# A gated two-layer block on one core: the alignment in two parts of 16 sequences, the second part's beside the first part's experts

## The chip, the cores and the metric

The kernel runs on one core of one Trainium2 chip. The time is device microseconds of one execution. Before the change three executions took 896.85, 896.81 and 893.13 us: the median is 896.81 us. The profiled execution took 894.79 us, of which 892.8 us lie between its first and its last instruction (the span); its mean granted TensorE clock is 0.857.

## What is computed

The input is 32 sequences of 128 tokens with 128 features. Two layers of two blocks follow, cut here to their core:

```python
x = x + tanh(g_xattn[0]) * mlstm(layernorm(x), ctx, ctx)       # 8 heads
x = x + tanh(g_ffn[0])   * qlinear(gelu(qlinear(layernorm(x), W1, b1)), W2, b2)
x = x + tanh(g_xattn[1]) * align(ctx, layernorm(x))
x = x + tanh(g_ffn[1])   * moe(layernorm(x))

def qlinear(x, W, b):      # both quantised to 8 bits over the WHOLE tensor
    xq, sx, zx = affine_quantize(x); wq, sw = sym_quantize(W)
    return (xq - zx) @ wq.T * (sx * sw) + b

def align(small, large):   # for each sequence by itself
    D = pairwise_euclidean(small, large)           # 128 x 128
    R[i, j] = D[i, j] + min(R[i-1, j], R[i, j-1], R[i-1, j-1])
    # walk back from the last corner; sum the rows of small met at each column
    return zeros_like(large).at[path_j].add(small[path_i])

def moe(x):                # 8 experts, all of them for every token
    logits = x @ gate.T
    kth = sort(logits.reshape(-1))[3072 - 1]       # over ALL 32 sequences
    gates = logits * (logits >= kth)
    y = gelu(x @ w1.T + b1) @ w2.T + b2            # per expert, 128 -> 512 -> 128
    return sum_e(gates[e] * y[e])
```

Two things couple the sequences. The scale of the second dense product needs the largest and smallest value of all of its inputs, and the gates need one threshold, the 3072nd smallest logit of all sequences. An expert's output for a token can be computed before the threshold is known, but it can only be weighted after it.

## The kernel before

A tile holds 128 tokens of a sequence on the 128 partitions, or its features. Sequences are taken in 8 groups of 4. The stages run in this order, each over all 32 sequences:

1. The first block (heads), then the first dense product. Its outputs after the gelu stay in `HT`, and their extremes give the scale of the second product.
2. The second dense product, `dense(n)` for group n. VectorE scales a block of 128x2048 (L865), ScalarE clips it from below (L868), VectorE from above (L869), TensorE makes 16 products into `po` (L874), and VectorE adds them to `X` (L879). Two groups at a time are then normalised (`norm_steps`) and turned (`tp`).
3. The distances, `take(g)`. ScalarE makes `ym2` and `ysq` (L884, L886), TensorE the squared distances `d2` (L888, L890), ScalarE adds a bias (L897) and takes the root (L899, L900), and DMAs put the rows into `d_dram` (L902).
4. The warp. A sequence is walked from both ends at once, so each of 64 partitions holds one half of one sequence and there are 64 rows of 128 columns. A row is two instructions on VectorE (L991, L992), one behind the other. Rows come in chunks of 16, 16, 16, 8 and 8, and the loads `dc` bring each chunk's distances. After a chunk its rows are spread by DMA over 128 partitions (`rblk`, two blocks of half a chunk), where five instructions find which way the path went (`dg`, `lf`, `to`, `vv` and `dv`, L1017 to L1029). `dv` goes back to 64 partitions by DMA (`DV`, L1031). ScalarE takes one part of it, a copy of the first column (L1028). At the last row the two halves meet (`meet`, L945 to L968), with two products on TensorE. Then 63 instructions `hit` (L1038) walk the path back, each needing the one before. `vt` and `ends` turn the result into the range of rows that each column takes.
5. The experts. `aligned(g)` adds the aligned context to group g (`ge`, `pt`, `px`), normalises it, turns it into `YT` (L1099) and computes its logits (L1102). A *unit* here means one group through one expert: 4 products `mph` of 128x512 (L1162), 4 gelus on ScalarE (L1165) and 16 products `mpo` of 128x128 (L1171). Groups are the outer loop, experts the inner one, 64 units in all. Groups 2 to 7 are aligned between the first units. The threshold is found bit by bit in 31 steps (`search`) among the units of group 1: each step is a count on VectorE, a product on TensorE (`small`, L1116) and three small instructions on VectorE. The outputs of groups 0 and 1 are held on chip (`ye`). From group 2 on `combine` adds each output to `X` with its gate: four instructions for the bias and four for the product, 128x128 each (L1150).

The weights of all 8 experts lie on chip (`mw1s` and `mw2s`, loaded at L751 and L752).

An instruction waits in its engine's queue behind those before it, and TensorE, VectorE and ScalarE take their queues in order. The order in a queue is the scheduler's, made when the kernel is built. `tc.issue_after(i)` only adds that what the block traces on i's engine stands behind i in that queue: it is no wait. DMAs that are issued from one engine stand in that engine's queue as well, and an issue waits there for the data, for the buffer, and for one of eight semaphores of the DMAs.

Of the kernel before, what the change touches and what calls it, by code (L numbers as in the profile page):

```python
# [18 lines left out]
P = 128  # L19
B = 32  # L20
# [14 lines left out]
CHUNKS = ((0, 16), (16, 16), (32, 16), (48, 8), (56, 8))  # L35


@with_exitstack
def tile_flamingo_gated(
# [23 lines left out]
    def pool(stack, name, bufs=1, space=None):  # L63
        kw = {} if space is None else {"space": space}
        return stack.enter_context(tc.tile_pool(name=name, bufs=bufs, **kw))
# [17 lines left out]
    w1s = new(keep, [P, HID], F32, "w1s")  # L83
    w2s = new(keep, [P, NC, D], F32, "w2s")
# [663 lines left out]
    late = pool(ctx, "late")  # L748
    mw1s = new(late, [P, E, HID], F32, "mw1s")
    mw2s = new(late, [P, E, NC, D], F32, "mw2s")  # L750
    nc.sync.dma_start(out=mw1s, in_=mw1)  # L751
    nc.sync.dma_start(out=mw2s, in_=mw2)  # L752


    aa_s = new(keep, [P, B], F32, "aa_s")
    d_dram = new(dram, [2, B, SH, S], F32, "d_dram")
    with ExitStack() as st:
        fp = pool(st, "ffn")
        HT = new(fp, [P, NC, B * S], F32, "HT")

        def lowest(lo, tag):

            low = new(fp, [P, 2], F32, tag)
            nc.vector.tensor_scalar(low[:, 1:2], lo, -1.0, None, ALU.mult)
            return low, nc.vector.tensor_scalar(low[:, 0:1], lo, MAGIC, None, ALU.subtract)
# [11 lines left out]
        with ExitStack() as st2:  # L777
            xp = pool(st2, "xq")
            p_h = pool(st2, "p_h", bufs=2, space=PSUM)
            cp = pool(st2, "context", bufs=2)  # L780
# [23 lines left out]
            for n in range(4):  # L804
                for c in range(NC):
# [7 lines left out]
                    hb = HT[:, c, 1024 * n : 1024 * n + 1024]  # L813
# [23 lines left out]
        aa = new(fp, [P, B], F32, "aa")  # L837
        with ExitStack() as st2:
            fps = pool(st2, "ffnps2", space=PSUM)
            mm = max_everywhere(fp, fps, hs2, 2, "mmh")  # L840
            sh, inv, lo, hi = affine_scale(fp, mm, "qh")
# [7 lines left out]
        s2 = new(fp, [P, 1], F32, "s2")  # L849
# [4 lines left out]
        ties = [tie, tie]  # L854


        dp = pool(st, "dist", bufs=2)
        lp = pool(st, "ln", bufs=2)
        p_o = pool(st, "p_o", bufs=2, space=PSUM)
        dps = pool(st, "distps", bufs=2, space=PSUM)  # L860

        def dense(n):
            blk = HT[:, :, 512 * n : 512 * n + 512]
            with tc.issue_after(getattr(ties[n], "ins", ties[n])):
                nc.vector.tensor_scalar(blk, blk, inv, MAGIC, ALU.mult, ALU.add)  # L865
            yield
            hq = new(dp, [P, NC, 512], BF16, "hqt")
            nc.scalar.activation(hq, blk, AF.Relu, bias=low[:, 1:2])  # L868
# [372 lines left out]
```

## Time and profile before

| | before |
|---|---|
| median of three executions | 896.81 us |
| profiled execution, its span | 894.79 us, 892.8 us |
| granted TensorE clock, mean | 0.857 |
| TensorE busy (matmuls) | 672.7 us, 75% of the span |
| VectorE busy | 548.7 us, 61% |
| ScalarE busy | 387.8 us, 43% |
| GpSimd busy | 19.4 us, 2% |
| HBM read, written | 14.01 MB, 4.46 MB |

Stages, by the timeline: the scaling of the second dense product starts at 226.5 us, its last distance DMA is issued at 287.9 us, the first row of the warp scans at 293.8 us and the last ends at 362.8 us, the walk back runs from 373.05 to 397.4 us, the first `mph` starts at 413.06 us and the last `mpo` ends at 888.3 us.

A busy share is read together with the stage that it belongs to: TensorE's 75% is an average over a stage in which it is nearly idle and one in which it never stops. In the lines of groups, "idle before" is the time that the engine stood still just before such an instruction, with what ended most of it.

### The profile page before, as it was taken

The numbers are of one execution on the slowest core, as the hardware profiler recorded it, in microseconds if no ns is written. First come the engines' busy times: TensorE is split into PE (matmuls) and PEld (weight loads), VectorE is DVE, ScalarE is ACT, GpSimd is POOL, SyncE is SP. The second block draws the span as 40 slices with busy tenths as digits, with TensorE's granted clock in tenths as the row PEclk, the third lists the DMA queues.
The fourth block names the chain that finished last, engine by engine and source line by source line (L and its number), as shares of the span: only waits on it lengthen the run. The fifth ranks groups of instructions, "written<-read, shape, count | busy, mean of one in ns | idle before, by whom it ended". The sixth has DMA issues, their size and how long they took to land.

```text
span 892.8 us, 12600 instructions
## 1 busy us (share of the span) xinstructions
PE 672.7 (75%) x4682; PEld 454.9 (51%) x4682; DVE 548.7 (61%) x1943; ACT 387.8 (43%) x672; POOL 19.4 (2%) x52
## 2 busy tenths in 40 slices
PE   5789998242475000017999999999999999999997
PEld 2244554110353000015777667777777777777776
DVE  7768988889882799786663556995222333222332
ACT  2788774595477000002443444334443344333342
POOL 2000000004000000000000000000000000000000
PEclk9899987555578555556999999999999999999999
DMA  8100000400013535100000000000000000000000
GB/s 314 35 2 12 2 2 1 189 0 0 1 24 72 126 85 113 42 0 1 1 1 1 1 1 1 13 1 25 1 13 1 1 12 1 12 1 1 13 1 12
DMA packets 11943, 25.32 MB, mean 28 GB/s; under 512 B 2386, under 2 KB 7250, under 8 KB 11090
## 3 DMA queue, kind: packets, MB, share of 16 engines
q1 hardware_dynamic: 9880, 20.19, 7.4%
q10 hardware_dynamic: 1874, 4.23, 2.1%
q8 instruction: 36, 0.59, 0.3%
q14 instruction: 25, 0.20, 0.1%
q0 software_dynamic: 128, 0.10, 0.0%
HBM read 14.01 MB, written 4.46 MB: 21 GB/s over the span
## 4 chain that ended last, share of the span: by engine, by line
PE 52%; DVE 21%; ACT 3%; issue 2%; DMA 1%; ACTq 0%; DVEq 0%; POOLq 0%
PE mpo L1171 25%; PE mph L1162 22%; DVE ru L992 3%; DVE hit L1038 3%; DVE hst L818 2%; DVE hst L819 2%; DVE ru L991 2%; PE d L888 1%; DVE bn L147 1%; PE d L890 1%; PE small L1102 1%; PE po L874 1%; DVE pt L1086 1%; ACT dd L897 1%; PE px L1089 1%
## 5 line engine op out<-in xcount | busy, mean ns | idle before, releaser
L1171 PEld LDWEIGHTS mpo<-mw2s,hT 128*128 128x128 f32 x2048 | 252.2, 192 | 62.5 <-issue 39.2
L1165 ACT ACTIVATE hT<-mph,mb1s 128x512 f32<-128x512 f32 x256 | 175.9, 687 | 238.4 <-PE mph L1162 236.7
L1171 PE MATMUL mpo<-mw2s,hT 128*128 128x128 f32 x2048 | 256.5, 276 | 0.1
L1162 PE MATMUL mph<-YT,mw1s 128*128 128x512 f32 x512 | 243.8, 599 | 0.0
L1150 DVE SCALAR_TENSOR_TENSOR X<-mpo,GA,X 128x128 f32<-128x128 f32 x192 | 54.0, 343 | 198.1 <-PE mpo L1171 198.1
L1162 PEld LDWEIGHTS mph<-YT,mw1s 128*128 128x128 f32 x512 | 87.8, 193 | 62.1 <-issue 62.0
L1150 DVE SCALAR_TENSOR_TENSOR X<-mb2s,GA,X 128x128 f32<-128x128 f32 x256 | 73.1, 342 | 0.0
L945 PE MATMUL gt_ps<-ident,ru 32*128 32x32 f32 x1 | 0.3, 283 | 78.3 <-DVE ru L992 78.3
L945 PEld LDWEIGHTS gt_ps<-ident,ru 32*128 32x128 f32 x1 | 0.2, 178 | 78.5 <-issue 78.5
L1028 ACT COPY dv<-vv 128x8 bf16<-128x8 bf16 (+1 forms) x5 | 1.1, 220 | 78.0 <-DMA rblk<-ru 48.3
L554 ACT ACTIVATE dm<-bi 128x512 f32<-128x512 f32 x48 | 28.7, 601 | 11.8 <-issue 4.2
L596 DVE TENSOR_TENSOR sm<-sc,dm 128x512 f32<-128x512 f32 x32 | 21.7, 684 | 13.3 <-ACT dm L554 9.3
L992 DVE TENSOR_TENSOR_SCAN ru<-ru,dc 64x128 f32<-64x128 f32 x64 | 26.6, 416 | 5.0 <-DMA dc<-d_dram 3.0
L809 PE MATMUL ph<-XQ,w1q 128*128 128x512 bf16 x32 | 15.4, 602 | 17.5 <-DVE XQ L800 9.5
L1099 ACT COPY YT<-px 128x512 f32<-128x512 f32 x8 | 4.7, 585 | 49.8 <-PE px L1098 49.8
L868 ACT ACTIVATE hqt<-HT,low 128x2048 bf16<-128x2048 f32 x8 | 15.8, 2000 | 22.2 <-DVE HT L865 14.0
L1179 ACT COPY ye<-mpo 128x512 f32<-128x512 f32 x16 | 9.4, 585 | 35.5 <-PE small L1116 18.1
L1044 PE MATMUL vt<-ident,vw 64*64 64x64 f32 x1 | 0.3, 312 | 32.3 <-DVE hit L1038 32.3
L1038 DVE SCALAR_TENSOR_TENSOR hit<-jotab,vw,DV 64x128 bf16<-64x128 bf16 x63 | 21.7, 344 | 4.6 <-DMA DV<-dv 2.4
L874 PE MATMUL po<-w2q,hqt 128*128 128x128 bf16 x128 | 13.4, 278 | 13.6 <-DVE hqt L869 13.6
L510 ACT ACTIVATE qm<-YT,mcol 128x512 f32<-128x512 f32 x32 | 23.1, 728 | 0.0
L147 DVE BATCH_NORM_STATS2 bn<-X 128x6 f32<-128x128 f32 x96 | 22.0, 280 | 0.1
(314 smaller groups left out, 912.1 us busy)
## 6 DMA issues: line engine op xcount, KB each, us to landing
X<-in_x SPq DMA_DIRECT2D x4, 512.0 KB, 6.1
CD<-in_ctx_d SPq DMA_DIRECT2D x4, 512.0 KB, 7.0
CT<-in_ctx_t SPq DMA_DIRECT2D x4, 512.0 KB, 9.2
mw1s<-in_mw SPq DMA_DIRECT2D x1, 2048.0 KB, 7.8
mw2s<-in_mw SPq DMA_DIRECT2D x1, 2048.0 KB, 12.2
out_x<-X SPq DMA_DIRECT2D x8, 256.0 KB, 2.0
d_dram<-dist SPq DMA_DIRECT2D x15, 128.0 KB, 2.4
rblk<-ru ACTq DMA_DIRECT2D x6, 297.0 KB, 4.3
```

The costliest lines, as they stand in the source:

```text
L147: nc.vector.bn_stats(bn[:, i, :], v[:, i, :])
L510: nc.scalar.activation(held["qm", g][:, h], YT[:, GB * g : GB * g + GB, :], AF.Copy, scale=mcol[:, h : h + 1],)
L554: done = nc.scalar.activation(dm, bi, AF.Exp)
L596: got = nc.vector.tensor_tensor(sm, scs[:, u], dm, ALU.mult)
L818: nc.vector.tensor_reduce(hst[:, 0, o : o + 1], hb, AX.X, ALU.max)
L874: nc.tensor.matmul(po[:, i, :], lhsT=hq[:, c, i * S : (i + 1) * S], rhs=w2q[:, c, :], start=(c == 0), stop=(c == NC - 1),)
L992: nc.vector.tensor_tensor_scan(ru[:, r + 1, 0, 1 : S + 1], u, dc[:, r, :], BIG, ALU.min, ALU.add)
L1038: nc.vector.scalar_tensor_tensor(hit, jotab[0:H2], vw[:, r + 1 : r + 2], DV[:, r, :], ALU.is_le, ALU.mult, accum_out=vw[:, r : r + 1],)
L1150: nc.vector.scalar_tensor_tensor(X[:, b, :], v, gate, X[:, b, :], ALU.mult, ALU.add)
L1162: nc.tensor.matmul(ph, lhsT=mw1s[:, e, c * P : (c + 1) * P], rhs=tok, start=True, stop=True)
L1165: nc.scalar.activation(hT[:, c, :], ph, AF.Gelu_apprx_tanh, bias=mb1s[:, e, c : c + 1])
L1171: nc.tensor.matmul(po[:, i, :], lhsT=hT[:, c, i * S : (i + 1) * S], rhs=mw2s[:, e, c, :], start=(c == 0), stop=(c == NC - 1),)
```

## The change

The 32 sequences are cut into two parts of 16 from the second dense product on. The first part goes through the second dense product, distances and warp, as before. Then the expert units begin with groups 0 to 3, and the second part's dense product, distances, warp, `aligned(4)` to `aligned(7)` and the search are put among them: a generator `background()` hands out these steps, and after each gelu and each output block of a unit `pump(0.85)` takes steps of about that many microseconds, by weights that are written beside each `yield`. The warp has as many rows and walk-back steps for 16 sequences as for 32, so there are two of them. The outputs of the first 36 units wait in DRAM (`y_dram`), with the bias already added by GpSimd, and are loaded again (`yl`) once the gates are known; from unit 36 on `combine` adds the bias to all four blocks at once and then does four instructions.

Other parts of it: expert weights come in pairs of experts through two buffers, and each pair is loaded twice (pair outer, groups inner). `rblk` has four blocks of a quarter of a chunk in place of two of a half, so the five instructions are half as long and the DMAs are twice as many. `DV` lies in `YT` or `CD`, and `DV` and `dc` are set to zero by GpSimd first. In the second part all of these DMAs are issued from SP, `po`, `tp` and `d2` share two banks of PSUM (`px`), and the roots of all four groups are two instructions of 64x2048.

```diff
+BP = B // 2
+NP = NG // 2
+BL = 4
+HELD = 36
...
-    mw1s = new(late, [P, E, HID], F32, "mw1s")
-    mw2s = new(late, [P, E, NC, D], F32, "mw2s")
-    nc.sync.dma_start(out=mw1s, in_=mw1)
-    nc.sync.dma_start(out=mw2s, in_=mw2)
+    def expert_weights(p):
+        w = new(late, [P, 2, HID], F32, "mw1"), new(late, [P, 2, NC, D], F32, "mw2")
+        for to, src in zip(w, (mw1, mw2)):
+            nc.sync.dma_start(out=to, in_=src[:, 2 * p : 2 * p + 2])
+        return w
+    weights = [expert_weights(0), expert_weights(1)]
...
+    def distances(s0, dd, dist, queues):
+        nc.scalar.activation(dist[0:SH], dd[0:SH], AF.Sqrt)
+        nc.scalar.activation(dist[SH:P], dd[SH:P, :, ::-1], AF.Sqrt)
...
+    def warp_steps(s0, n_s, wp, w1p, ps_new, queues, DV, ends):
+        nc.gpsimd.memset(DV, 0.0)
+        dcs = [new(w1p, [H2, 16, S], F32, f"dc{k}") for k in range(2)]
+        for dc in dcs:
+            nc.gpsimd.memset(dc, 0.0)
...
-            m = n // 2
-            rb = new(w1p, [P, 9, 2, S + 4], F32, "rblk")
-            for q in range(2):
+            m = n // BL
+            rb = new(w1p, [P, 16 // BL + 1, 2, S + 4], F32, "rblk")
+            for q in range(BL):
                 for h in range(2):
+                    at = 2 * n_s * q + n_s * h
                     queues[h].dma_start(
-                        out=rb[H2 * q + B * h : H2 * q + B * h + B, 0 : m + 1],
-                        in_=ru[B * h : B * h + B, q * m : q * m + m + 1],
+                        out=rb[at : at + n_s, 0 : m + 1],
+                        in_=ru[B * h : B * h + n_s, q * m : q * m + m + 1],
                     )
...
+        def second_part():
...
+                for w in dense_steps(1, held["aligned", NP - 1], dp, lpB, px_new, p_x, "px", take):
+                    yield w
+                distances(BP, dd, dist, (nc.sync, nc.sync))
+                yield 2.0
...
+                for w in warp_steps(
+                    BP, BP, wp, w1p, lambda shape, tag: new(p_k, shape, F32, "small"),
+                    (nc.sync, nc.sync), DV, ends[1],
+                ):
+                    yield w
+            for g in range(NP, NG):
+                for w in aligned(g):
+                    yield w
+            for w in search():
+                yield w
...
+        def pump(more):
+            time[0] += more
+            while time[0] > 0:
+                with ExitStack() as ties:
+                    for k in ("mm", "gelu"):
+                        ties.enter_context(tc.issue_after(held[k]))
+                    w = next(steps, None)
+                if w is None:
+                    return
+                time[0] -= w
...
+        def combine_early():
+            g, e, k = early.pop(0)
+            yl = new(yp, [P, GB, D], F32, "yl")
+            nc.sync.dma_start(out=yl, in_=y_dram[k])
+            combine(g, e, yl, True)
...
+        units = [
+            (k, p, g, j)
+            for k in range(2) for p in range(E // 2) for g in range(NP * k, NP * k + NP) for j in range(2)
+        ]
+        for n, (k, p, g, j) in enumerate(units):
...
+            if n < HELD:
+                ye = new(yp, [P, GB, D], F32, "ye")
+                nc.scalar.copy(ye, po)
+                nc.gpsimd.tensor_add(ye, ye, mb2s[:, e : e + 1, :].to_broadcast([P, GB, D]))
+                nc.sync.dma_start(out=y_dram[n], in_=ye)
+                early.append((g, e, n))
+            else:
+                until("GA")
+                for _ in range(-(-len(early) // (len(units) - n))):
+                    combine_early()
+                combine(g, e, po, False)
+            if g % NP == NP - 1 and j == 1:
+                weights.pop(0)
+                if n + 2 * NP < len(units) - 1:
+                    weights.append(expert_weights((p + 2) % (E // 2)))
```

## The prediction

> **What bounds the kernel now.** I read the time slices first, then the busy times of four stretches, then the groups, the timeline around the places where work will move, and last the order in which the built program of the changed kernel has its instructions in each queue (it holds no times).
>
> ```profile
> PE   5789998242475000017999999999999999999997
> DVE  7768988889882799786663556995222333222332
> PEclk9899987555578555556999999999999999999999
> ```
> ```profile
> 226.00:290.00 64.00, 38.24 (x240) 29.10 (x240) 43.35 (x156) 43.75 (x73) 0.72 (x5) 0.71 0.16 33
> 290.00:373.00 83.00, 0.92 (x3) 0.36 (x3) 69.84 (x168) 1.54 (x7) 0.86 (x7) 0.50 0.45 99
> 373.00:400.00 27.00, 1.53 (x6) 1.10 (x6) 23.42 (x134) 0.00 (x0) 0.00 (x0) 0.50 0.00 1
> 620.00:700.00 80.00, 80.00 (x466) 58.74 (x465) 23.17 (x86) 30.68 (x45) 0.00 (x0) 1.00 0.01 4
> ```
> Columns of the stretches: length, busy us of TensorE, its weight loads, VectorE, ScalarE, GpSimd, granted clock, DMA share, GB/s. VectorE alone sets the pace from 290 to 400 us, TensorE alone from 413 us: 80.00 of 80.00 us busy at clock 1.00. The expert stage is a wall: a unit recurs every 7.006 us (573.36, 580.37, 587.38 in the chain), so 64 units are 448.4 us of the 475.1 between 413.06 and 888.2. Whatever moves into this stage must fit beside TensorE, and whatever TensorE does for it is added in full.
>
> **Ahead of the experts: what goes.** (a) Half of the second dense product and distances. Eight groups take 226.5 to 287.9. I replay the first four with these rows: a scaling 1.28, `hqt` on ScalarE 2.00 and VectorE 0.75, two `d2` from 248.81 to 254.25 at the half clock, the rest as in the timeline. Up to 241 us nothing changes; then VectorE loses 1.9 us of groups 4 and 5, the second pair no longer waits for 2.00 us pieces of `hqt`, and the last root ends at about 265.9. **−22.0.**
>
> (b) The first part's warp has its 64 rows, 0.78 us each, and its 63 `hit` unchanged. Its block instructions halve: for 16 rows 1.19+1.21+0.68+2.28+0.68 = 6.0 become the 3.3 that 8 rows cost today (0.68+0.67+0.41+1.19+0.41). Three chunks save 2.7 each, and the fourth chunk's block now stands behind the last row: rows end 11.1 earlier. But the meeting gets longer:
> ```profile
> 362.87 0.52 ACTq L1002 DMA_DIRECT2D rblk<-ru  x1
> 362.99 0.28 PE L945 MATMUL gt_ps<-ident,ru 32*128 32x32 f32 x1 [78.30 <-DVE ru L992]
> 370.75 0.51 ACTq L1031 DMA_DIRECT2D DV<-dv  x1
> 373.05 0.34 DVE L1038 SCALAR_TENSOR_TENSOR hit<-jotab,vw,DV 64x128 bf16<-64x128 bf16 x1 [2.39 <-DMA DV<-dv]
> ```
> Today the last `rblk` is issued as the rows end, and the first `hit` starts 10.1 us later. In the new order `rblk` has one buffer still, and the last chunk's eight DMAs may only start when the fourth chunk's `lf` has read it, some 3.9 us after the last row; among them, on both queues, stand four `DV` issues that wait for `dv` (about 6 us). With 0.51 an issue they are out at 8.9, land 2.4 later, the last block takes 2.2, four more `DV` issues 2.0 and 2.0 to land: first `hit` at 17.5. +7.4, so **−3.7** (ends: −11, if the meeting hides it all, and +4).
>
> (c) `aligned(1)` leaves the start: its products stand between 410.3 and 413.06, of which 0.9 go. **−0.9.** GpSimd's clearing of `DV` (8192 values; 0.94 for 1024, so 7.5) stands ahead of the 9.25 us of bias added to `X` at 213.97; it then ends at 230.8, and the first reader is at 233.65. Hidden by 2.8 us.
>
> **Beside the experts: what comes.** (d) TensorE's own part of the second dense product: per group 16 `po` 0.95 (row at 254.25: 1.06), four turns 0.55, `d2` 0.86 and 0.9 (starts at 282.77 and 283.63), 3.4 in all. Four groups: **+13.6.** Nothing can hide it.
>
> (e) ScalarE in units 4 to 8 of the new order: 16 gelus of 0.69, four `hqt` of 2.0, eight `ym`/`ysq` of 0.5, 16 biases of 0.26, the roots and the copies: 37 us in some 42 of TensorE's. It fits, but gelus queue behind it. Worst at unit 8: biases 1.0, table load, two roots of 64x2048 (2.1 each, as 128x2048 costs 2.00), a copy 0.5, a table load, then the next gelu.
> ```profile
> 253.65 2.02 ACT L868 ACTIVATE hqt<-HT,low 128x2048 bf16<-128x2048 f32 x1
> 255.68 1.28 ACT L899 ACT_TABLE_LOAD   x1
> 256.97 0.63 ACT L899 ACTIVATE dist<-dd 64x512 f32<-64x512 f32 x1
> ```
> That is 9 us without a gelu; `mph` has three buffers, so TensorE has 1.8+2.6 us of work and stands 4.8. The Trainium skill (ScalarE: Activation LUTs, What ACT_TABLE_LOAD costs) speaks against such a pair of switches: each is 1.28 of load plus 1.38 of drain, 2.66. Here the root starts 1.29 after the load began and `hqt` had ended before, so I see no drain and take 1.28; by the rule the wait would be 7.5. For the other queueing I take 2.8 (0 to 8). **+7.6.**
>
> (f) The second warp is placed from unit 9 to unit 27. VectorE's work there would fit, but all DMAs now stand in SP's queue in a fixed order: eight `rblk`, the next `dc`, eight `DV`, with `y_dram` stores between. Each `DV` waits for a ScalarE copy that stands at gelu 13.25, 17.5, 20.5, 22.5 and 23.5 (in units); behind the third `DV` stand the fourth `rblk` and, behind it, the last `dc`. From the roots' end at unit 8 (time 0): third copy 89.4, eight `DV` 93.4, eight `rblk` 97.4, `dc` lands 100.9, eight rows and a block: 107.8. TensorE reaches the meeting's first product (its place is unit 23.25) at 103.4 and waits 4.4; ScalarE's queue waits with it. From there to the first `hit`: 12.5 (today's 10.1, plus four more issues); walk 24.5; TensorE has 89 `mpo` of 0.223 and 15 `mph` of 0.86, 33.8 with the meeting, and waits 3.8 more at `vt`. **+8.2** (0 to 30).
>
> (g) One more aligned group in the stage (2.9, by 9.93 against 7.006 for a unit with one, less 1.4 already there): +1.5. The search costs 0.72 a unit today over 8 units; in the new order five steps stand in a unit and some follow after 1.12 us where the steps at 499.99 and 501.46 need 1.47: +0.8. From `ends` to the first `px`: +1.5. **+3.8.**
>
> (h) Held outputs: 33 loads come right after the search, up to 4.75 between two `combine`. 4.75 times 1.06 for four instructions, plus 0.74 and 1.06, is 6.8 of 7.0 us; with three buffers and 2.0 to land a load recurs after about 1.35, so 8.1. PSUM holds two outputs, so I take +2.0 (0 to 8); at the end 0.7 for the separate bias. **+2.7.** Stores on SP, GpSimd's 1.16 an addition (half of 2.3) and the weights (512 KB every 28 us) lie beside the 7 us units.
>
> (i) Waits of 4.8, 4.4 and 3.8 us let the clock fall. The first eight `mph` passes after the idle stretch took 5.29, a later eight 3.60:
> ```profile
> 413.06 5.29 PE L1162 MATMUL mph<-YT,mw1s 128*128 128x512 f32 x8
> 424.25 3.60 PE L1162 MATMUL mph<-YT,mw1s 128*128 128x512 f32 x8
> ```
> So about 1.8 to warm up. The Trainium skill (TensorE: Matmul & The Clock Gate, HAM oscillation) speaks against idle gaps of over 3.4 us between products: by it all three are followed by slow products, +5.5. The rows are less regular: `d2` ran slow for three pieces after an idle 2.18 (at 261.72) and 3.06 us (272.00), but not after 2.35 (280.92). I count two of the three, **+3.7** (0 to 8, as shorter waits can cost it too).
>
> **Sum.** −26.6 ahead, 13.6+7.6+8.2+3.8+2.7+3.7 = +39.6 beside: **+13.0** on the profiled 894.79, 907.8; from the median of 896.81, 0.2% higher, it is 909.8. Forecast **908**. The change moves 62 us of dense work and a warp, but the warp is as long for 16 as for 32, so only half of the dense stage leaves the front.
>
> **Rivals.** *It is hidden* (faster): the second part's chain stays ahead of its places, TensorE never waits for VectorE, and the first warp keeps all it saves. For: VectorE is idle for over half of the expert stage. Against: SP's fixed order. −22.0−9.4−0.9, then 13.6+2.6+2.3+0.7: −13, 882. It decides if the meeting's first product waits less than 1 us.
> *It cancels*: half the waits of (e), (f) and (h), no warming up, and 7 saved in (b): −29.9+13.6+3.8+4.1+3.8+1.7 = −2.9, about 892 to 899.
> *TensorE follows the chain* (slower still): a chunk of the second warp is served one step after another, 12.5 rows, eight issues, 2.4, 3.3, eight issues = 26.4, three times; the short ones 18.8; meeting 12, walk 24.5, first loads 10: 163 us, unit 31.3 in place of 27: 30 us in place of 8.2, so 930. It decides if `rblk` starts only after the rows.
> *Nothing moves*: excluded, the order has the second part's warp among units 9 to 27.
>
> **Numbers.** My forecast 0.54 (898 to 920), hidden 0.13, cancels 0.16, follows 0.17. 890 to 930 leaves most of the first and half of the last out, about 0.2. About 0.5% is what this measurement can tell from no change: faster 0.14, same 0.17, slower 0.69.
>
> **What would show it.** First row of the warp about 22 us earlier; first `hit` about 17 after the last row; first `mph` near 386; a ScalarE stretch of 9 us without a gelu near unit 8 with TensorE idle for 5; TensorE waiting for `ru` at the meeting and for `hit` at `vt`; 7.0 us per unit elsewhere. A wait at `vt` over 20, or none at all, makes it wrong.

## The result, and the profile after

The changed kernel takes **918.26 us** (median of 4 runs, 916.10 to 919.86) against 894.98 for the kernel before (893.13 to 896.85): a ratio of **1.026** with a 95% interval from 1.022 to 1.030. It is slower. The profiled execution took 916.10 us with a span of 914.4; before, 894.79 and 892.8. The sum of the prediction was +13.0 on these profiled executions; measured is +21.3, so 8 us are to be explained, beside the 13 that were foreseen.

The time slices of the page after, in 40 slices of 22.9 us each:

```profile
PE   5789997242630000399979999897999999999997
DVE  7768999799819967766615665597866788222242
PEclk9898998555675555599999999897999999999999
```

The wall of nines in TensorE's row starts two slices sooner than before. But it has dents now (a seven, an eight, another seven), and at the last two of them, slices 26 and 28, the granted clock falls to 8 and 7 tenths. VectorE's row is down to 2 and 4 only in the last six slices.

The busy time in stretches of the changed kernel; columns as in the prediction (length, busy us of TensorE, weight loads, VectorE, ScalarE, GpSimd, granted clock, DMA share, GB/s):

```profile
265.40:348.60 83.20, 0.92 (x3) 0.36 (x3) 60.09 (x169) 1.47 (x7) 4.36 (x9) 0.51 0.39 57
427.50:484.50 57.00, 51.77 (x322) 37.62 (x321) 23.96 (x76) 37.48 (x57) 17.56 (x13) 0.94 0.23 62
577.00:633.00 56.00, 46.59 (x261) 36.79 (x262) 38.51 (x168) 17.52 (x30) 9.76 (x8) 0.85 0.29 94
712.50:908.00 195.50, 195.39 (x1118) 141.94 (x1118) 90.62 (x294) 76.86 (x112) 1.27 (x1) 1.00 0.22 67
```

The loss sits in the middle of the expert stage. The third row, around the second warp's meeting and walk, has TensorE idle for 9.4 of 56 us and its clock at 0.85. The last row, with 36 held outputs coming back, has no gap at all: 195.39 of 195.50 busy at clock 1.00.

The timeline of the first part's meeting, and after it TensorE's at the start of three places in the expert stage (roots, second meeting, second walk's end):

```profile
331.41 0.28 PE L962 MATMUL gt_ps<-ident,ru 32*128 32x32 f32 x1 [69.12 <-DVE ru L1010]
338.54 1.22 SPq L1021 DMA_DIRECT2D rblk<-ru  x2
344.70 2.68 ACTq L1054 DMA_DIRECT2D YT<-dv  x4
348.61 0.34 DVE L1063 SCALAR_TENSOR_TENSOR hit<-jotab,vw,YT 64x128 bf16<-64x128 bf16 x1 [4.00 <-DMA YT<-dv]
```
```profile
387.46 2.05 PE L1323 MATMUL mph<-YT,mw 128*128 128x512 f32 x2
...
477.22 2.07 PE L1323 MATMUL mph<-YT,mw 128*128 128x512 f32 x2 [4.64 <-ACT hT L1328]
479.09 5.37 PE L1336 MATMUL mpo<-mw,hT 128*128 128x128 f32 x32
...
578.63 0.28 PE L962 MATMUL small<-ident,ru 32*128 32x32 f32 x1 [4.38 <-DVE ru L1010]
...
622.99 0.31 PE L1070 MATMUL small<-ident,vw 64*64 64x64 f32 x1 [7.78 <-DVE hit L1063]
```

The last number in brackets is how long TensorE stood. The first `mph` comes at 387.46, 25.6 us sooner than before (413.06). Then TensorE stands 4.6 us for a gelu behind the roots (4.8 was predicted), 4.4 for the last row at the meeting (4.4 predicted) and 7.8 for the walk (3.8 predicted). Why the walk was longer than 24.5 us is seen in the timeline of VectorE and GpSimd inside it:

```profile
598.99 0.34 DVE L1063 SCALAR_TENSOR_TENSOR hit<-jotab,vw,CD 64x128 bf16<-64x128 bf16 x1
...
599.36 1.27 POOL L1345 TENSOR_TENSOR ye<-ye,mb2s 128x512 f32<-128x512 f32 x1 [1.72 <-ACT ye L1344]
599.38 1.39 DVE L1063 SCALAR_TENSOR_TENSOR hit<-jotab,vw,CD 64x128 bf16<-64x128 bf16 x1
600.82 0.34 DVE L1063 SCALAR_TENSOR_TENSOR hit<-jotab,vw,CD 64x128 bf16<-64x128 bf16 x1
```

A `hit` takes 0.34 us. The one that starts 0.02 after GpSimd's addition of the expert bias takes 1.39 and ends 0.14 after it. Four of the 63 are caught so. This is where the theory of the experiments comes from: **the 36 additions that the change puts on GpSimd hold up VectorE**, on whose chain TensorE waits. The rivals: the second warp waits for SyncE's queue, for ScalarE's queue, or for its places in TensorE's order.

### The profile page after: what moved, and what is told of

Same layout as the page of the kernel before. It is cut to its first block, busy times and chain, and to the rows that moved or that the text cites. A ratio compares the mean times of both kernels' runs of the same rounds, so it can differ in the third digit from the quotient of the medians.

```text
span 914.4 us, 13331 instructions
## 1 busy us (share of the span) xinstructions
PE 679.4 (74%) x4691; PEld 456.3 (50%) x4691; DVE 598.0 (65%) x2013; ACT 398.5 (44%) x695; POOL 89.7 (10%) x107
## 4 chain that ended last, share of the span: by engine, by line
PE 43%; DVE 25%; ACT 4%; DMA 3%; issue 3%; SPq 2%; ACTq 0%; DVEq 0%; POOL 0%
PE mpo L1336 18%; PE mph L1323 18%; DVE hit L1063 5%; DVE ru L1010 3%; DVE ru L1009 2%; DVE hst L842 2%; DVE hst L843 2%; DMA rblk<-ru 2%; SPq L1054 1%; PE px L1151 1%; DVE bn L154 1%; PE small L1170 1%; PE px L1165 1%; DVE junk L1184 1%; DVE root_t L187 1%
## 5 line engine op out<-in xcount | busy, mean ns | idle before, releaser
L1336 PEld LDWEIGHTS mpo<-mw,hT 128*128 128x128 f32 x2048 | 251.9, 195 | 50.3 <-issue 31.4
L1336 PE MATMUL mpo<-mw,hT 128*128 128x128 f32 x2048 | 259.8, 280 | 0.1
L1323 PE MATMUL mph<-YT,mw 128*128 128x512 f32 x512 | 243.1, 600 | 4.6 <-ACT hT L1328 4.6
L1323 PEld LDWEIGHTS mph<-YT,mw 128*128 128x128 f32 x512 | 88.8, 194 | 70.2 <-issue 64.0
L1345 POOL TENSOR_TENSOR ye<-ye,mb2s 128x512 f32<-128x512 f32 x36 | 46.9, 1306 | 314.2 <-ACT ye L1344 311.7
L1010 DVE TENSOR_TENSOR_SCAN ru<-ru,dc 64x128 f32<-64x128 f32 x128 | 56.4, 441 | 12.2 <-DMA dc<-d_dram 8.1
L1293 DVE SCALAR_TENSOR_TENSOR X<-yl,GA,X 128x128 f32<-128x128 f32 x144 | 40.1, 345 | 8.9 <-DMA yl<-y_dram 8.8
L1009 DVE TENSOR_TENSOR ru<-ru 64x128 f32<-64x128 f32 x128 | 39.8, 311 | 4.6
L1293 DVE SCALAR_TENSOR_TENSOR X<-biased,GA,X 128x128 f32<-128x128 f32 x112 | 31.9, 347 | 0.7
L1063 DVE SCALAR_TENSOR_TENSOR hit<-jotab,vw,CD 64x128 bf16<-64x128 bf16 x63 | 25.7, 407 | 8.4 <-DMA CD<-dv 6.2
L603 DVE TENSOR_TENSOR sm<-sc,dm 128x512 f32<-128x512 f32 x32 | 21.7, 683 | 13.3 <-ACT dm L561 9.7
L833 PE MATMUL ph<-XQ,w1q 128*128 128x512 bf16 x32 | 15.0, 590 | 17.9 <-DVE XQ L824 10.2
L1063 DVE SCALAR_TENSOR_TENSOR hit<-jotab,vw,YT 64x128 bf16<-64x128 bf16 x63 | 21.7, 344 | 6.2 <-DMA YT<-dv 4.0
```

Source lines behind the costliest of these rows:

```text
L603: got = nc.vector.tensor_tensor(sm, scs[:, u], dm, ALU.mult)
L1009: nc.vector.tensor_tensor(u, ru[:, r, 0, 1 : S + 1], ru[:, r, 0, 0:S], ALU.min)
L1010: nc.vector.tensor_tensor_scan(ru[:, r + 1, 0, 1 : S + 1], u, dc[:, r, :], BIG, ALU.min, ALU.add)
L1063: nc.vector.scalar_tensor_tensor(hit, jotab[0:H2], vw[:, r + 1 : r + 2], DV[:, r, :], ALU.is_le, ALU.mult, accum_out=vw[:, r : r + 1],)
L1293: nc.vector.scalar_tensor_tensor(X[:, b, :], y[:, i, :], GA[:, E * b + e : E * b + e + 1], X[:, b, :], ALU.mult, ALU.add,)
L1323: got = nc.tensor.matmul(ph, lhsT=w1e[:, j, c * P : (c + 1) * P], rhs=tok, start=True, stop=True)
```

## The experiments

One table first. "First mph" is when the expert stage begins. "Excess" is the span from there to its end, less 64 units of 7.006 us (448.4); before the change it was 892.8 − 413.1 − 448.4 = 31.3. (The expectation of e8 counts only to the last `mpo`, some 5 us less.) Then TensorE's three waits in us. All of it is from each run's own profile, the time is the median of its timed runs. Each run's ratio is to the kernel before on the same chip.

| kernel | first mph | excess | roots | meeting | vt | time | ratio (95%) |
|---|---|---|---|---|---|---|---|
| changed | 387.5 | 78.5 | 4.6 | 4.4 | 7.8 | 918.3 | 1.026 (1.022 to 1.030) |
| e1 no bias addition | 387.6 | 68.3 | 4.6 | 3.5 | 3.4 | 908.0 | 1.013 (1.007 to 1.018) |
| e2 bias by VectorE | 392.3 | 74.6 | 4.5 | 0.9 | 2.3 | 916.3 | 1.019 (1.013 to 1.025) |
| e3 no table loads | 387.4 | 78.7 | 2.1 | 3.4 | 8.3 | 917.3 | 1.022 (1.017 to 1.027) |
| e4 later places | 390.2 | 81.1 | 4.6 | 4.4 | 8.6 | 919.5 | 1.024 (1.018 to 1.029) |
| e5 bias added late | 388.9 | 66.7 | 4.6 | 3.5 | 1.5 | 906.6 | 1.013 (1.009 to 1.017) |
| e6 weights on ScalarE's queue | 387.5 | 82.0 | 5.1 | 3.9 | 9.6 | 924.1 | 1.035 (1.029 to 1.041) |
| e7 later places 2 | 387.8 | 71.8 | 4.6 | none | none | 912.1 | 1.019 (1.014 to 1.023) |
| e8 combined | 388.0 | 59.4 | 2.4 | 1.7 | none | 899.7 | 1.004 (1.001 to 1.006) |
| e9 two row buffers | 385.1 | 79.1 | 4.6 | 4.4 | 7.2 | 914.5 | 1.020 (1.017 to 1.022) |
| e10 combined, two buffers | 383.2 | 61.9 | 2.4 | 1.7 | none | 896.4 | 0.999 (0.997 to 1.002) |
| e11 dense in front | 405.9 | 54.1 | none | none | 4.2 | 908.8 | 1.013 (1.009 to 1.016) |
| e12 warp alone, remedied | 402.7 | 42.7 | none | none | 1.3 | 893.3 | 0.997 (0.994 to 1.000) |

The first mph moves by up to 5 us from one execution to another with nothing changed ahead of it (e2, e4), so the excess tells more of the stage than the time does. The three columns do not hold all waits: TensorE also stood for the copy of an output (3.0 us in e3, 2.6 in e5, 3.6 in e10), for what is told below in e2 and e7, and for a `y` of VectorE (2.2 and 3.0 in e11, 2.2 in e12).

**e1: the bias addition left out.**

```diff
                 nc.scalar.copy(ye, po)
-                nc.gpsimd.tensor_add(ye, ye, mb2s[:, e : e + 1, :].to_broadcast([P, GB, D]))
```

> GpSimd's 36 additions of the expert bias to held outputs are left out (so the bias of these outputs is missing from the result). Theory A: a VectorE instruction that meets a GpSimd addition stands for the whole 1.3 us of it; four hits did, so the hits fall from 25.7 to 21.7 us, the wait at vt falls from 7.8 to about 3.8 and the scans of the second warp lose their 24 ns each, which shortens the meeting's wait from 4.4 to 2 to 4; the time is 4 to 7 us below the changed kernel's 918, about 912. Rival B: the hits are slowed by something else (transfers, PSUM reads) and the wait at vt comes from the queue of transfers: it stays between 7 and 8.5 and the time stays within 2 us of 918.

The time fell by 10 us, more than theory A's 4 to 7. The wait at `vt` fell to 3.4 as it said, the one at the meeting to 3.5. Rival B falls. In the traces VectorE and ScalarE run the same instructions in the same order as in the changed kernel, so it is not a new order that gained the time. But here work is missing, so the same without loss:

**e5: the bias added late, by VectorE.**

```diff
             yl = new(yp, [P, GB, D], F32, "yl")
             nc.sync.dma_start(out=yl, in_=y_dram[k])
-            combine(g, e, yl, True)
+            combine(g, e, yl, False)
...
-                nc.gpsimd.tensor_add(ye, ye, mb2s[:, e : e + 1, :].to_broadcast([P, GB, D]))
```

> The 36 GpSimd additions go, but nothing is left out: a held output is stored without its bias, and VectorE adds the bias (0.74 each, 27 us in all) after loading it back, in the late units, where it was busy 27 of 91 us. Theory A (the additions cost some 10 us as they stand among VectorE's work, as e1_no_bias_add says): the same waits as there (3.5 at the meeting, 3.4 at vt, no aligned transpose waiting for y), late units still 7.0 each with at most 3 us lost where two to four held outputs stand between two direct ones: 908 to 911. Rival B (what e1_no_bias_add gained came from work left out at the end): 915 to 919.

906.6, with nothing left out: what e1 gained was not the missing work. VectorE's groups from 480 to 640 us, first of the changed kernel, then of e5 (busy us, mean ns of one; idle us before them):

```profile
L1010 DVE TENSOR_TENSOR_SCAN ru<-ru,dc 64x128 f32<-64x128 f32 x64 | 29.7, 464 | 6.2 <-DMA dc<-d_dram 4.1
L1063 DVE SCALAR_TENSOR_TENSOR hit<-jotab,vw,CD 64x128 bf16<-64x128 bf16 x63 | 25.7, 407 | 8.4 <-DMA CD<-dv 6.2
L1009 DVE TENSOR_TENSOR ru<-ru 64x128 f32<-64x128 f32 x63 | 21.4, 340 | 2.4
```
```profile
L1010 DVE TENSOR_TENSOR_SCAN ru<-ru,dc 64x128 f32<-64x128 f32 x64 | 26.7, 417 | 6.4 <-DMA dc<-d_dram 4.4
L1063 DVE SCALAR_TENSOR_TENSOR hit<-jotab,vw,CD 64x128 bf16<-64x128 bf16 x63 | 21.7, 344 | 9.1 <-DMA CD<-dv 6.9
L1009 DVE TENSOR_TENSOR ru<-ru 64x128 f32<-64x128 f32 x63 | 17.9, 284 | 2.4
```

Same instructions, same counts: 3.0 us of scans, 4.0 of hits and 3.5 of row minima (L1009) come back. That is time of the instructions themselves. The idle time before them is no smaller in e5 (6.4 and 9.1 us for 6.2 and 8.4), so the gain is not that transfers came sooner once the stores of outputs no longer waited for GpSimd. TensorE's side of it, e5 around the walk's end:

```profile
618.42 0.24 PE L1070 MATMUL small<-ident,vw 64*64 64x64 f32 x1 [1.46 <-DVE hit L1063]
...
618.65 1.16 PE L1336 MATMUL mpo<-mw,hT 128*128 128x128 f32 x8
```

After a wait of 1.46 us the next eight `mpo` passes take 1.16. After 7.78 us in the changed kernel they took 2.07. The shorter wait saves its slow products too.

**e2: the bias added by VectorE as the output leaves PSUM.**

```diff
-                nc.scalar.copy(ye, po)
-                nc.gpsimd.tensor_add(ye, ye, mb2s[:, e : e + 1, :].to_broadcast([P, GB, D]))
+                nc.vector.tensor_tensor(
+                    ye, po, mb2s[:, e : e + 1, :].to_broadcast([P, GB, D]), ALU.add
+                )
```

> Held outputs leave PSUM by one VectorE addition with the bias, in place of a ScalarE copy and a GpSimd addition: nothing is left out. Theory A: no stalled hits, but 3 to 4 additions of 0.74 stand among the walk and some 12 more among the rows, so the wait at vt is 6 to 7.5 and the one at the meeting 4 to 7; ScalarE is relieved of 0.5 a unit; in all 0 to 3 us below 918. Rival B (GpSimd's additions cost nothing): 2 to 6 us above 918, by the added VectorE work on the second warp's chain.

Neither theory's details hold. The waits at the meeting and at `vt` fall to 0.9 and 2.3, but TensorE now stands three times (1.8, 3.0 and 3.0 us) for a PSUM buffer that the addition frees, since the addition queues behind VectorE's warp. The excess is 3.9 smaller; the time (916.3) says little, as its first `mph` came 5 us late. So it matters to whom the addition is given, and late is better than early.

**e3: the two table loads taken away.**

```diff
-    def distances(s0, dd, dist, queues):
+    def distances(s0, dd, dist, queues, root=AF.Sqrt):
...
-                distances(BP, dd, dist, (nc.sync, nc.sync))
+                distances(BP, dd, dist, (nc.sync, nc.sync), AF.Copy)
```

> The second part's two roots on ScalarE become copies of the same shapes, so the two table loads around them go; distances of the second part are then squares. Theory A (a load costs its own 1.28 and no drain): the wait of TensorE at unit 8 falls from 4.6 by 2.6 to about 2.0, and the slow products after it (5.37 for 32 where 3.7 is usual, 3 to 3.5 us in all with the mph beside them) stay or shrink by half; the time is 3 to 5 us below 918. Rival B (1.28 of load plus 1.38 of drain each, the skill's figure): the wait falls by 4.6 to 5.3, to nothing, the slow products go too, and the time is 7 to 8 us below 918.

Timeline of TensorE in e3, at the roots and ahead of the meeting:

```profile
475.21 1.12 PE L1323 MATMUL mph<-YT,mw 128*128 128x512 f32 x2 [2.06 <-ACT hT L1328]
...
572.09 3.06 PE L1336 MATMUL mpo<-mw,hT 128*128 128x128 f32 x14 [2.99 <-ACT ye L1344]
578.55 0.22 PE L962 MATMUL small<-ident,ru 32*128 32x32 f32 x1 [3.40 <-DVE ru L1010]
```

The wait fell from 4.64 to 2.06, by 2.58: twice 1.28 and nothing more, so no drain was paid with the loads, as the prediction took it. No slow products follow 2.06 us (1.12 for the two `mph` passes in place of 2.07). But the time gained at unit 8, 3.6 us with the slow products, was gone again at the meeting. The second warp's rows came no sooner: the meeting's product starts at 578.55, and at 578.63 in the changed kernel. Ahead of it ScalarE, with a copy of `dv` at the head of its queue, stood 4.1 us for `vv` of VectorE, and TensorE 2.99 for the copy of an output behind it. What is won ahead of a chain that something else paces is not won.

**e4 and e7: the meeting's products and vt placed later.** The edit of e4; e7 has 36.0 in place of 6.0, holds 42, and does it in the second part alone:

```diff
-HELD = 36
+HELD = 40
...
             if last:
+                yield 6.0
                 meet(ru[:, n, 0, 1 : S + 1])
...
+        yield 9.0
         vt = ps_new([SH, 2, H2], "vt")
```

> The meeting's products are placed 6 us of work later and vt another 9 later in the order beside the experts, and 40 outputs are held in place of 36 so that the search may end later; nothing is left out. Theory A (TensorE only waits because these products were placed ahead of VectorE's chain): waits of 4.4 and 7.8 fall under 1 each, the slow products behind them (about 1.9 each) go, and nothing comes back, since held loads have room: 13 to 16 us below 918, about 903. Rival B (the chain itself is what bounds: its delay is handed to aligned groups and the search, and TensorE stands at the search's end or at the first product of the second part instead): at most 5 us below 918, with a new wait of over 5 us between 640 and 760. Rival C (ScalarE's queue is what the second warp waits for, so that a later place makes the chain itself later): waits at the meeting and at vt stay over 3 each.

The waits stayed over 3, which is rival C's sign, but this was no test of it or of the others: the built order of e4 has both products after the same number of outputs as before (20.4 and 26.0 in units), so nothing was moved and the waits stayed; the excess is 2.6 larger, 0.8 of it at `vt`, and the rest is not explained. The program writes the meeting in unit 16 and `vt` in unit 21; the planner had already put them four to five units later, by its own times of the work that they wait for. A later written place counts only beyond that.

> As e4_later_places, but with 36 us of work ahead of the meeting (and 9 ahead of vt, 42 held outputs), since there the built order had kept both products at the same outputs (20.4 and 26.0 in units): here they stand at 21.25 and 28.0. Theory A (TensorE waits because the products stand ahead of VectorE's chain): the wait at the meeting falls from 4.4 to under 1, the one at vt from 7.8 to under 1, slow products behind them go: 10 to 15 us below 918. Rival B (the chain bounds, the delay is handed on): a new wait of over 5 us at the first product of the second part, or units over 8.1 while the search runs, and at most 5 us below 918.

With 36 us the products do move, by 0.8 and 2 units, and both waits are gone, as theory A says. The gain is 6 us where 10 to 15 were expected, because TensorE stands elsewhere. TensorE in e7:

```profile
582.08 1.72 PE L1325 MATMUL mph<-YT,mw 128*128 128x512 f32 x2 [2.12 <-DMA mw<-in_mw]
587.27 2.08 PE L1338 MATMUL mpo<-mw,hT 128*128 128x128 f32 x8 [3.46 <-ACT ye L1346]
```

The new weights are late by 2.1 us. The copy of an output, late by 3.5, waits for the store of an earlier one, and that is issued at 584.28 behind the second warp's rows in SyncE's queue. Rival B's wait at the second part's first product did not come.

**e6: the weight loads on ScalarE's queue.** In the changed kernel the chain that ended last, taken between 577 and 595 us, runs through a weight load, and only then through the rows of the warp's last block:

```profile
577.46 5.68 DMA mw<-in_mw
583.16 2.08 DMA rblk<-ru
...
592.73 1.74 DMA CD<-dv
```

```diff
-    def expert_weights(p):
+    def expert_weights(p, queue=None):
...
-            nc.sync.dma_start(out=to, in_=src[:, 2 * p : 2 * p + 2])
+            (queue or nc.sync).dma_start(out=to, in_=src[:, 2 * p : 2 * p + 2])
...
-                    weights.append(expert_weights((p + 2) % (E // 2)))
+                    weights.append(expert_weights((p + 2) % (E // 2), nc.scalar))
```

> The weight loads inside the expert stage are issued from ScalarE's queue in place of SyncE's; all else stays. In the changed kernel the last block's rows of the second warp landed only 2.08 us after a weight load of 5.68 that stands just ahead of them in SyncE's queue. Theory A (transfers of one queue land one after the other): the last block lands 5 to 6 us sooner after the meeting, the first hit follows the meeting's product by about 12 in place of 17.5, the wait at vt falls from 7.8 to 2 to 3, and the time is 4 to 6 us below 918. Rival B (the landing is set by the transfer engines, which the load fills from any queue): first hit still 16 or more after the meeting, wait at vt 7 or more, time within 2 us of 918.

The short rows now land in 2.1 to 2.2 us each in place of up to 5.4, which is theory A, and VectorE has the last `dv` 6.9 us after the meeting's product, in place of 9.7 (there an addition held it: 1.17 us in place of 0.29). Still the first `hit` comes 16.6 us after the meeting's product (15.9 before the edit), which is rival B's number, though not by its reason. The chain that ended last in e6, and the `hit`:

```profile
586.54 4.20 DMA mw<-in_mw
590.74 0.02 issue
590.76 0.51 SPq L1054
...
593.84 1.73 DMA CD<-dv
```
```profile
595.66 0.35 DVE L1063 SCALAR_TENSOR_TENSOR hit<-jotab,vw,CD 64x128 bf16<-64x128 bf16 x1 [9.68 <-DMA CD<-dv]
```

Two waits ate the gain. The transfers need a ScalarE copy of `dv`, which starts only at 587.46 (587.18 in the changed kernel), 1.5 us after VectorE's `dv`. Of the eight transfers two go out then, and the third stands 1.9 us until 590.76, when the weight load that ScalarE had issued has landed. All eight carry the same `dv` to the same buffer; what differs is the semaphore that each issue waits for, and the third's was the load's. So the load had left SyncE's queue and still held it up. Why the excess grew by 3.5, and the time by 6, is not settled beyond that; three waits of 1.0 to 1.2 us for `y` among the second aligned groups are a part.

**e9: two buffers for the rows' copy.**

```diff
-            rb = new(w1p, [P, 16 // BL + 1, 2, S + 4], F32, "rblk")
+            rb = new(w1p, [P, 16 // BL + 1, 2, S + 4], F32, "rblk", bufs=2)
```

> The rows' copy for the blocks (rblk) gets two buffers in place of one, in both parts; nothing is left out. Theory A (the last chunk's eight transfers wait for the fourth chunk's lf to have read the one buffer): in the first part the time from the last row to the first hit falls from 17.3 to about 13.5, and the first mph comes at about 383.5 in place of 387.5; the time is 3 to 5 us below the changed kernel's 918. Rival B (the issues themselves, 0.51 to 0.6 each on two queues with the DV issues among them that wait for dv, are what takes the time): 16 or more from the last row to the first hit, time within 2 us of 918.

From the meeting's product to the first `hit`, in the profile of e9:

```profile
335.67 0.28 PE L962 MATMUL gt_ps<-ident,ru 32*128 32x32 f32 x1 [71.26 <-DVE ru L1010]
...
346.23 0.34 DVE L1063 SCALAR_TENSOR_TENSOR hit<-jotab,vw,YT 64x128 bf16<-64x128 bf16 x1 [4.04 <-DMA YT<-dv]
```

10.6 us in place of 17.2. A part of that is work that now stands ahead of the last row (from the first scan, at 275.06, to the meeting's product it took 60.6 us in place of 58.9). First row to first hit is 71.2 in place of 76.1. Theory A: one buffer cost 4.9 us.

**e11: the second part's dense work back in front.** `dense_steps(1, ...)` runs right after `dense_steps(0, ...)`, with the same pools, and leaves `second_part`:

```diff
             0, held["quantized"], dp, lp, lambda: new(p_o, [P, GB, D], F32, "po"), dps, "tp", take
         ):
             pass
+        for _ in dense_steps(
+            1, held["quantized"], dp, lp, lambda: new(p_o, [P, GB, D], F32, "po"), dps, "tp", take
+        ):
+            pass
     parts[0].close()
+    parts[1].close()
```

> One part of the change is undone: the second part's dense product, norms and distances run ahead of the experts again, right after the first part's; only its warp stays beside the experts. Theory A (what left the front comes back among the experts in full: TensorE's own 13.4, the 4.6 behind the roots and 3 to 4 of slow products): first mph 21 to 23 us later, about 409.5; units 4 to 9 take 7.0 each, so 22 to 23 us less there; the time is within 3 us of 918. Rival B (the dense work beside the experts is a true gain, the loss is the second warp alone): 925 or more. Rival C (the dense work beside also delays the second warp through ScalarE's queue): the waits at the meeting and at vt fall as well, 910 or less.

The first `mph` comes 18.5 us later (not 22, since the second part's dense work now runs on beside the first rows of the warp, which start at 278.6), the excess is 24.4 smaller, and the time is 908.8: rival C. So this half of the change lost by itself. Taking four groups of dense work out of the front saved 18 us there, and cost 24 among the experts. Of these 14.0 are their own products, 4.6 the wait behind the roots and some 3 the slow products after it. The waits at the meeting and at `vt` are 8.0 shorter in e11, and new ones for a `y` (2.2 and 3.0) stand against that. In e11 the meeting's product does not wait.

**e8, e10 and e12: the remedies together.** e8 has the edits of e5, e6 and e7 and issues the second part's roots behind the last gelu of a unit; e10 adds e9. e12 is e11 with the edits of e5 and e9.

```diff
+                while held["slot"] != NC - 1:
+                    yield 0.85
                 distances(BP, dd, dist, (nc.sync, nc.sync))
...
                 held["gelu"] = getattr(got, "ins", got)
+                held["slot"] = c
...
                 held["mm"] = getattr(got, "ins", got)
+                held["slot"] = -1
                 pump(0.85)
             if n < HELD:
```

> All remedies at once, nothing left out: bias of held outputs added late by VectorE, weight loads on ScalarE's queue, the second part's roots issued right after the last gelu of a unit (TensorE then has 3.6 of mpo and 2.6 of mph to do beside the 7 us of loads and roots), later places as in e7_later_places_2. Theory A (each wait is a local one): no wait of TensorE over 1.5 us in the expert stage, excess over 64 units of 7.0 about 46 to 52 us in place of 72; time 893 to 900, about the kernel before. Rival B (waits only move): 905 or more, with a wait over 5 us somewhere from 600 to 720.

> e8_combined with the two row buffers of e9_two_row_buffers. Theory A (the gains add up, as the one lies ahead of the expert stage and the others within): 894 to 897, that is 3 to 5 below e8_combined and about the kernel before. Rival B: 899 to 901, as e8_combined.

> Only the second part's warp beside the experts, as in e11_dense_in_front, with the bias of held outputs added late by VectorE (e5_bias_late) and two row buffers (e9_two_row_buffers); nothing is left out, places as the order has them. Theory A (GpSimd's additions cost here what they cost there, about 10, and the buffer 4): 894 to 898, level with the kernel before, with the wait at vt under 1. Rival B (with the dense work gone from the stage VectorE has more time and the additions meet less of it): 900 to 905. If A holds, moving the dense work among the experts is worth nothing even with every wait repaired, since e10_combined_two_row_buffers stands at 896.

e8 came out at 899.7 and e10 at 896.4, as their theories A had it, though two waits of e8 stayed over the 1.5 us that theory A allowed (2.4 behind the roots, 1.7 at the meeting) and its excess to the last `mpo` was 54 where at most 52 was expected. With every remedy the whole change is level with the kernel before: 0.999, from 0.997 to 1.002. e12, which moves only the warp and takes two small edits, is at **893.3: 0.997, from 0.994 to 1.000**, at the edge of what this measurement can tell, and with 1.3 at `vt` where theory A wanted under 1. It is 3 us below e10, but the two intervals overlap. The clock and the busy time of two stretches of its expert stage, one with the second warp's later rows and walk, one from 640 us on:

```profile
448.30:562.00 113.70, 112.93 (x638) 81.00 (x636) 57.08 (x219) 53.95 (x87) 0.52 (x4) 1.00 0.33 91
640.00:888.00 248.00, 247.67 (x1423) 180.21 (x1422) 113.59 (x348) 100.79 (x148) 0.00 (x0) 1.00 0.20 62
```

TensorE is busy for 112.93 of 113.70 us while VectorE does 57 us beside it, nearly all for the second warp. That is the change as it was hoped for, with GpSimd out of the way. Its longer waits lie outside these stretches: 2.2 us at 441 and 1.3 at 562.

## Why the prediction was right or wrong

The direction, the likeliest case and the range held (908 forecast, 898 to 920 as the likeliest case, 890 to 930 as the range; 918.3 measured, near the upper end of the likeliest). The sum was 8.6 us short in span (+13.0 against +21.6). Term by term, from the two profiles:

| term | predicted | measured | where it is read |
|---|---|---|---|
| (a) half of the dense work leaves the front | −22.0 | −22.6 | last distance transfer issued at 265.31, before at 287.93 |
| (b) first warp | −3.7 | −1.8 | rows −10.3, meeting +7.1, before the first row +1.3 |
| (c) start of the stage | −0.9 | −1.2 | first hit to first mph, 38.9 for 40.0 |
| (d) TensorE's own dense work | +13.6 | +14.0 | four units from 427.5 to 470.0, less a wait of 0.5 |
| (e) ScalarE's queue | +7.6 | +5.2 | waits of 4.64, and of 0.54 for a `y` of VectorE |
| (f) second warp | +8.2 | +12.2 | waits of 4.38 and 7.78 |
| (g) aligned groups, search | +3.8 | +6.2 | not measured: what is left of +47.2 (excess 78.5 for 31.3) |
| (h) held outputs | +2.7 | +0.7 | nothing in the units, 0.7 in the tail (5.2 for 4.5) |
| (i) slow products | +3.7 | +8.9 | about 3 after each of the three waits |

**The step that failed is a clause in (h)**: GpSimd's addition was put "beside the 7 us units", that is, at nothing but its own time on an idle engine. It costs 10 to 12 us: 10.2 of excess in e1 and 11.8 in e5, and as much of the time. That is more than the whole miss. It is spread over four terms. In (f), hits and rows are longer: with the additions gone the two waits are 4.9 in place of 12.2, below the 8.2 predicted. In (g), aligned groups: TensorE waited 3.3 us in five places for a `y` of VectorE, and 0.3 in e5. In (e), the 0.54: that `y` began during an addition and took 1.18 us in place of 0.34. In (i), because shorter waits leave fewer slow products. The sum had no upper price for the additions, though each runs beside VectorE's chain.

The Trainium skill has the rule (SBUF — State Buffer, section SBUF: two separate sides): a port pair is shared by VectorE and GpSimd as an exclusive lock for a whole instruction, taken by whichever starts first, and of VectorE's instructions it concerns those with two SBUF inputs, against a GpSimd operation that reads SBUF, and those in a two-port mode. The trace agrees in the main. Matching all of VectorE's instructions in the stage with the additions, 20 that began during one (a `hit` 0.05 us ahead of it) were about 1.0 us too long each, 19 us in all. Sixteen of them have two operands in SBUF. Four have one tensor operand (`y` twice, a block of `HT`, a small step of the norm), and the trace does not say whether they ran in a two-port mode. Others already running when an addition began, and all of the search (PSUM or one operand), lost nothing. By the rule a price could have been set before: nearly all of the second warp's 66 us on VectorE (scans 26.7, hits 21.7, row minima 17.9, as e5 has them) has two SBUF inputs, and an addition of some 1.2 us comes every 7.

Two smaller sizes were off. In **(i)** I counted two of three waits as cold; all three were, and each cost about 3 rather than 1.85 (the two rows it was taken from give 1.69). In **(b)** a cost was overlooked: the warp now fills only half of the partitions of `dc`, so GpSimd clears it first. The first clearing starts at 268.55 and takes 1.8; only then, at 270.38, is the first transfer into `dc` issued, and the first row comes 7.2 us after the last distance transfer in place of 5.9. The meeting itself was right to 0.2 us (17.35 from the end of the last row, predicted 17.5), and its reason, the one buffer of `rblk`, is shown by e9, though the buffer cost 4.9 and not the 3.9 I had for it. The rows gained 10.3 of the 11.1.

What was right for the reason given: (a) and (d); the wait behind the roots, with no drain beside the loads (e3); units of 7.0 us elsewhere; the search, at 8.0 a unit. Held outputs came back without a gap, where 2.0 (0 to 8) had been put.

In (f) the sizes came out better than the steps behind them. The wait at the meeting was 4.4 to the tenth, as the difference of two times after the roots' end that were both too late: 107.8 for VectorE's rows and 103.4 for TensorE, where the trace has 104.1 and 99.7. It also holds 0.9 of the additions (3.5 in e5). So the tenth was luck. At `vt`, 12.5 + 24.5 less 33.8 is 3.2 and not 3.8. From the meeting's product to the first `hit` were 15.9 us where 12.5 was put. That is not the additions' doing (16.9 in e5) nor the one buffer's (15.8 in e9). The weight load ahead of the rows in SyncE's queue has a part, as e6 shows, but a shorter landing alone brought the `hit` no nearer, since ScalarE's copy and the load's semaphore came next; so a fixed order of one queue is not the only cause. No run relieved all of them at once and nothing else.

The rival "it is hidden" needed the meeting to wait less than 1 us, and it waited 4.4; e7 brought that about and gained 6, not the 26 between that rival and the forecast, since TensorE then stood for two other things. "It cancels" had the waits halved and no slow products; there were 8.9 us of them. "TensorE follows the chain" put the second warp's delay at 30 us; the two waits came to 12.2, and a wait over 20 at `vt`, the sign that was named, was not there.

## What to carry to other kernels

An engine that is idle is not free: ask which port, queue or buffer its new work shares with the engine on the critical chain, and set an upper price for it. Before moving work beside a saturated engine, compare what leaves the front (here 18 to 23 us of dense work) with what that engine must do for it in full (14 us), plus one stall and one slow stretch at every point where it waits for the moved chain. Here no form of the change was clearly faster: all of it with every remedy came out level, and the warp alone, which needs almost no TensorE, at 0.997. And a place written later in the program moves nothing until the built order moves: read that first.

## What the hardware showed that was not expected

- A GpSimd addition of two SBUF operands (1.27 us) stops a VectorE instruction with two SBUF operands that begins during it until it has ended (1.39 in place of 0.34). Four with one tensor operand were held as well (a `y` 1.18 in place of 0.34), while those of the search ran through.
- How long TensorE may stand before its products slow down has no one answer here. After 1.46 (e5) and 2.06 us (e3) none were slow; after 2.12 (e7) two `mph` passes took 1.72 where 1.02 is usual, so slow products came after less than the 3.4 of the rule weighed in the prediction. But in the kernel before, a wait of 2.35 (at 280.92) left none, and e8 and e10 part after the same wait and the same next products:

```profile
581.44 0.22 PE L962 MATMUL small<-ident,ru 32*128 32x32 f32 x1 [1.66 <-DVE ru L1010]
...
582.97 4.54 PE L1327 MATMUL mph<-YT,mw 128*128 128x512 f32 x6
```
```profile
576.70 0.21 PE L962 MATMUL small<-ident,ru 32*128 32x32 f32 x1 [1.67 <-DVE ru L1010]
...
578.23 2.84 PE L1327 MATMUL mph<-YT,mw 128*128 128x512 f32 x6
```

  In e8 (first) the granted clock falls to 0.50 from 584 to 586 us, some 2 us after TensorE had started again; in e10 it stays at 1.00 over these products. The length of the stand does not decide alone; what else does was not tested.
- A DMA issue can wait for a transfer of another engine: in e6 SyncE stood 1.9 us for the landing of a weight load issued by ScalarE.
- A wait of 2.6 us that was taken out (e3) moved nothing at the next meeting, 100 us later, to within 0.1 us.
